# FP4 weights and rotary tables prepared beside the first scan, and a second stage whose tiles wait tile by tile

## Chip, cores and metric

The kernel runs on one core of a Trainium2 chip. A core has TensorE (PE, with its weight loads counted as PEld), VectorE (DVE), ScalarE (ACT), GpSimd (POOL) and a queue for transfers on SyncE (SP); ACT issues some transfers too. The metric is the device time of one execution in microseconds. The time before is the median of three runs; the profile is of one more execution.

## The reference, cut to what matters

The input is eight sequences of 512 tokens with 256 channels. Two layers follow each other. The first normalizes x and adds a selective state-space scan and a feed-forward net, whose inputs, weights and hidden values are quantized to FP4 in blocks of 16. The second normalizes again and adds a block-sparse attention with 16 heads and a two-layer local-attention transformer, whose queries and keys are scaled and rotated.

```python
xn = _layernorm(x)
x = x + scan(xn) + fp4_ffn(xn)                 # stage 1
xn = _layernorm(x)
x = x + sparse_attention(xn) + local_transformer(xn)   # stage 2

def step(h, inp):                              # 512 steps, state 512 x 16
    d_t, u_t, B_t, C_t = inp
    dA = jnp.exp(d_t[:, :, None] * A[None])
    h = dA * h + (d_t * u_t)[:, :, None] * B_t[:, None, :]
    return h, jnp.einsum('bdn,bn->bd', h, C_t)

def fp4_linear(x, w):                          # x @ quantized(w).T
    return jnp.einsum('bsk,nk->bsn', fp4_quant_dequant(x), fp4_quant_dequant(w))

def fp4_quant_dequant(x):                      # blocks of 16 along the last dim
    scale = jnp.maximum(jnp.max(jnp.abs(xb), -1, keepdims=True) / 6.0, 1e-12)
    return _GRID[jnp.searchsorted(_MID, jnp.abs(xb / scale))] * sign(xb) * scale

q, k = l2norm(q) * q_scale, l2norm(k) * k_scale
q = q * cos * scale + rotate_half(q) * sin * scale
k = k * cos / scale + rotate_half(k) * sin / scale
```

## The kernel before

The whole program is one launch of two stages, and each stage goes through the eight sequences (batches) one after the other. The result of stage 1 goes to a DRAM tile per batch (x1_d, stored on ACT's queue at L369), and stage 2 loads it again (load_x1, L390). All data is float32. A batch lies in tiles of 128 tokens x 256 channels, or, turned, of 128 channels x 512 tokens.

The Python program emits the instructions of all engines in one order that is written by hand; the framework then lists each engine's instructions, mostly in that order, and an engine takes its own list in order. Where two strands of work run side by side, they are generators, and `beside` (L111) takes a step of the second strand whenever its share of steps is behind that of the first. Tiles come from rotating pools. A tile that takes the bytes of an earlier one waits for the earlier one's users; the framework puts in these waits, and so a transfer's start can hang on work that has nothing else to do with it.

**Before the first scan.** The weights of stage 1 are loaded on SP's queue (`load`, L134). Then the FP4 weights are made (L177 to L213). The gate and up weights (704 x 256 each) come in four chunks each of 88 rows x 512 values, loaded on ACT's queue into q_src (two buffers). The down weight comes in two chunks of 128 x 704. `fp4` (L81) quantizes a chunk in ten instructions: on DVE the blocks' maximum (L96), the scale (L97), its reciprocal (L98, L100), on POOL the scaling (L101), on ACT the power-of-two step (L105), on DVE three more (L106 to L108), and on POOL the scaling back (L109). PE turns a chunk into a PSUM tile (ps_w at L186, ps_i at L202), and DVE or ACT, in turns, copy it out (`evac`, L46). Then head(0) runs.

**head(b)** (L218) loads x, normalizes it, turns it (xt), and computes for four channel chunks the input product (ps_in), the convolution (cv, one L235 and three L239 on DVE) and its Silu on ACT (u). Then it computes the products that give B and C (ps_xp, copied to xd at L250 and stored to a DRAM tile bc_d on SP's queue, L252), and for each chunk the step size delta and du (a softplus chain over ACT, DVE at L267 and L268, and POOL at L270 to L272).

**scan(b)** (L323) goes through two pairs of channel chunks and, in each, 16 states. For a state, one transfer spreads B and C over the partitions (bc, L330). For each chunk of the pair, ACT makes da in PSUM (L338), DVE multiplies du with B (hh, L340) and runs the recurrence over the 512 tokens in one instruction (L341), POOL multiplies with C (L342), and PE adds the states up in a PSUM bank (y, L343). After a pair, the output is gated (DVE L355, POOL L358); after both, PE projects it (ps_o, L364), DVE adds it to xs (L368) and xs is stored (L369).

**ffn(b)** (L276) quantizes xn (one chunk for two token tiles), and for each of the four token tiles computes the gate and up products, quantizes the hidden tile h (704 wide), turns it and multiplies with the down weight (L317), and adds it to x in xs (L320).

Beside each scan run ffn of the same batch and head of the next:

```python
for b in range(NB):
    rest = [ffn(b)] + ([head(b + 1)] if b + 1 < NB else [])
    beside(scan(b), chain(*rest), 34, 24)
```

So 34 steps of the scan carry 24 other steps.

**Stage 2** opens seven new pools (L380 to L386) over the space of stage 1's. SP's queue then issues, in the order of the program: wq, wk, wv, their biases, wao, bsum (to which POOL adds a bias at L403), the mask (L419; POOL fills other tiles before it, and DVE casts the mask in eight copies at L422 and L423), and for each of the two transformer layers the rotary table (512 KB, tab at L432), the two scales (qs, L435), 26 small DVE instructions that multiply them (L437 and L440 to L442), a store of the product to a DRAM tile (L444) and four small loads. `fetch` (L453) then loads the first transformer weights (wqkv, tab, wo, wf1, wf2, 5204 KB), and only then does the first proj load x1s_0.

**proj(b)** (L489) normalizes a batch (statistics at L496 and L497, the scaled values at L500), turns it to s0, and computes queries and keys of the sparse attention (ps_qk L514, copied to qt and kt by DVE at L518) and the values (ps_v L524, bias added at L529). **smax** (L535) computes the scores once (ps_s L557 and L559) to take row maxima on DVE (nm, L563 and L565). qkv, attn and ffn of the transformer and st and outer of the sparse attention follow. The order ahead of the first of them is:

```python
fetch(0, 0, "wqkv", "tab", "wo", "wf1", "wf2")
tc.keep_in_program_order(act.preload_act_table_set("natural_log_exp_and_others"))
alone(proj(0))
alone(smax(0, 0))
```

Of the kernel before, what the change touches and what calls it, by code (L numbers as in the profile page):

```python
# [38 lines left out]
def tile_kernel(ctx: ExitStack, tc: tile.TileContext, a: dict, out: bass.AP):  # L39
# [99 lines left out]
    def chunks(w):  # L139
        return w.rearrange("(k p) n -> p k n", p=P)  # L140
# [4 lines left out]
    with ExitStack() as s0:  # L145
# [28 lines left out]
        w_g = w0.tile([P, KC, FI], FP, name="w_g")  # L174
        w_u = w0.tile([P, KC, FI], FP, name="w_u")
        w_d = w0.tile([P, NI, D], FP, name="w_d")
        for name, dst in (("w_gate", w_g), ("w_up", w_u)):  # L177
            src = a[name].rearrange("(j p) d -> p j d", p=FB)
            for j in range(0, FI // FB, 2):
                raw = q.tile([P, FI], FP, tag="q_src", name="q_src")[:FB, : 2 * D]  # L180
                act.dma_start(raw.rearrange("p (j d) -> p j d", j=2), src[:, j : j + 2, :])
                fp4(raw, raw, FB, 2 * D, q, sm)
                ps = pmm.tile([P, L], FP, tag="mm", name="ps_w")
                for k in range(KC):
                    for i in range(2):
                        pe.transpose(  # L186
                            ps[:, (2 * k + i) * FB : (2 * k + i + 1) * FB],
                            raw[:, i * D + k * P : i * D + (k + 1) * P],
                            ident[:FB, :FB],
                        )  # L190
                evac(
                    dst[:, :, j * FB : (j + 2) * FB],
                    ps[:, : 4 * FB].rearrange("p (k n) -> p k n", k=KC),
                )

        def inner_to_partitions(src, dst):

            for c0, c1 in ((0, 4), (4, NI)):
                ps = pmm.tile([P, L], FP, tag="mm", name="ps_i")
                for c in range(c0, c1):  # L200
                    n = min(P, FI - c * P)
                    pe.transpose(ps[:n, (c - c0) * P : (c - c0 + 1) * P], src[:, c * P : c * P + n], ident)  # L202
                full = c1 - c0 - (c1 * P > FI)
                evac(dst[:, c0 : c0 + full, :], ps[:, : full * P].rearrange("p (c n) -> p c n", n=P))
                if c0 + full < c1:
                    n = FI - (c1 - 1) * P
                    evac(dst[:n, c1 - 1, :], ps[:n, full * P : (full + 1) * P])

        for r in range(D // P):
            raw = q.tile([P, FI], FP, tag="q_src", name="q_src")  # L210
            act.dma_start(raw, a["w_down"][r * P : (r + 1) * P, :])
            fp4(raw, raw, P, FI, q, sm)
            inner_to_partitions(raw, w_d[:, :, r * P : (r + 1) * P])  # L213


        made = {}
# [156 lines left out]
            pass  # L373
        for b in range(NB):
            rest = [ffn(b)] + ([head(b + 1)] if b + 1 < NB else [])
            beside(scan(b), chain(*rest), 34, 24)


    with ExitStack() as s1:
        w0 = s1.enter_context(tc.tile_pool(name="w1", bufs=1))  # L380
        w1 = s1.enter_context(tc.tile_pool(name="io1", bufs=2))
        sm = s1.enter_context(tc.tile_pool(name="sm1", bufs=4))
        one = s1.enter_context(tc.tile_pool(name="one1", bufs=1))
        rot = s1.enter_context(tc.tile_pool(name="rot1", bufs=2))
        pmm = s1.enter_context(tc.tile_pool(name="pmm1", bufs=6, space=PSUM))
        po = s1.enter_context(tc.tile_pool(name="po1", bufs=2, space=PSUM))  # L386

        def load_x1(b):
            t = w1.tile([P, NT, D], FP, tag="x1", name=f"x1s_{b}")
            sp.dma_start(t, x1_d[b])  # L390
            return t

        wq = load(w0, chunks(a["wq"]), [P, KC, NH * HP], "wq")
        wk = load(w0, chunks(a["wk"]), [P, KC, NH * HP], "wk")
        wv = load(w0, chunks(a["wv"]), [P, KC, D], "wv")
# [30 lines left out]
            "wqkv": [P, KC, 3 * IN], "tab": [P, 4, NT, LD], "wo": [P, IN // P, D],  # L426
            "wf1": [P, KC, 2 * HID], "wf2": [P, NHC, D],
        }
        lng, lnb, b1, b2c, tab_d = [], [], [], [], []
        for l in range(DEPTH):  # L430
            tab = one.tile(shapes["tab"], FP, tag="tab", name="tab")
            sp.dma_start(tab, a["rotary"])  # L432
            for i, name in ((0, "q_scale"), (2, "k_scale")):
                qs = sm.tile([P, LD], FP, tag="qs", bufs=2, name="qs")
                sp.dma_start(qs, a[name][l].unsqueeze(0).to_broadcast([P, LD]))  # L435
                if i == 0:
                    dve.tensor_scalar(qs, qs, 8.0, None, ALU.mult)  # L437
                hd = LD // 2
                for t in range(NT):
                    dve.tensor_tensor(tab[:, i, t, :], tab[:, i, t, :], qs, ALU.mult)  # L440
                    dve.tensor_tensor(tab[:, i + 1, t, :hd], tab[:, i + 1, t, :hd], qs[:, hd:], ALU.mult)
                    dve.tensor_tensor(tab[:, i + 1, t, hd:], tab[:, i + 1, t, hd:], qs[:, :hd], ALU.mult)  # L442
            tab_d.append(dram.tile(shapes["tab"], FP, tag=f"tab_{l}", bufs=1, name=f"tab_{l}"))
# [43 lines left out]
        x1s, ss_, bs = {}, {}, {}  # L487

        def proj(b):  # L489
            x1 = x1s[b] = load_x1(b)  # L490
            xn = one.tile([P, NT, D], FP, tag="hn", name="xn")
            st = sm.tile([P, NT, 6], FP, tag="ln_st", bufs=2, name="ln_st")
            mv = sm.tile([P, NT, 2], FP, tag="ln_mv", bufs=2, name="ln_mv")
            rs = sm.tile([P, NT], FP, tag="ln_rs", bufs=2, name="ln_rs")
            for t in range(NT):
                dve.bn_stats(st[:, t, :], x1[:, t, :])  # L496
                dve.bn_aggr(mv[:, t, :], st[:, t, :])  # L497
            inv_sqrt(rs, mv[:, :, 1], eps_t)
            for t in range(NT):
                dve.tensor_scalar(  # L500
                    xn[:, t, :], x1[:, t, :], mv[:, t, 0:1], rs[:, t : t + 1], ALU.subtract, ALU.mult
                )
            yield
            s = ss_[b] = stream("s0", "s0")
            to_channels(xn, s[:, :, S0:], pmm, "mm")
            yield
            qt = one.tile([P, 4, L], FP, tag="bqt", name="qt")
            kt = one.tile([P, 4, L], FP, tag="bkt", name="kt")
            bs[b] = qt, kt
            for dst, wt, bias, sc in ((qt, wq, bq, 0.25), (kt, wk, bk, 1.0)):  # L510
                for c in range(4):
                    ps = pmm.tile([P, L], FP, tag="mm", name="ps_qk")
                    for k in range(KC):
                        pe.matmul(  # L514
                            ps, wt[:, k, c * P : (c + 1) * P], s[:, k, S0:],
                            start=(k == 0), stop=(k == KC - 1),
                        )
                    dve.tensor_scalar(dst[:, c, :], ps, bias[:, c : c + 1], sc, ALU.add, ALU.mult)  # L518
                    yield
            for t in range(0, NT, 2):  # L520
                ps = pmm.tile([P, L], FP, tag="mm", name="ps_v")
                for i in range(2):
                    for k in range(KC):
                        pe.matmul(  # L524
                            ps[:, i * D : (i + 1) * D], s[:, k, S0 + (t + i) * P : S0 + (t + i + 1) * P], wv[:, k, :],
                            start=(k == 0), stop=(k == KC - 1),
                        )
                for i in range(2):
                    dve.tensor_tensor(  # L529
                        bv_t[:, t + i, :, :HD], ps[:, i * D : (i + 1) * D].rearrange("p (h d) -> p h d", d=HD),  # L530
                        bv.rearrange("p (h d) -> p h d", d=HD), ALU.add,
                    )
                yield
# [465 lines left out]
```

## Time and profile before

| | |
|---|---|
| median of 3 runs | 4184.37 us (4177.97 to 4188.32) |
| the profiled execution | 4182.33 us, of which the span of its instructions is 4180.5 us |
| PE / PEld busy | 3488.5 us (83%) / 1700.7 us (41%) |
| DVE busy | 2892.1 us (69%) |
| ACT busy | 1721.5 us (41%) |
| POOL busy | 1456.9 us (35%) |
| mean granted PE clock | 0.883 of full speed |
| moved by DMA | 239.27 MB, mean 57 GB/s |

The busy share is a mean over stages that differ. The page's second part cuts the span into 40 slices of 104.5 us and gives each engine's busy share in tenths: DVE's digits are 9 from the third to the seventeenth slice, where PE's are 7, and from the nineteenth slice on PE's are 9 (8 in two) while DVE's are 4 to 6. So each stage is read for itself. In a row of the groups, the line number says where the instruction is written, "out<-in" names the tiles, xN counts instructions, then come their busy time and mean duration, and last the engine's idle time just before them and what ended it. In the chain of waits, each row is what the next one waited for, with its start and duration in microseconds. In the list of issues (part 6), the last number is the median time from a transfer's issue to its landing. The first 106.2 us pass before the first scan instruction, the eight scans take until 1808, and the first matmul of stage 2 follows at about 1848.

### The profile page before, as it was taken

Reading aid. Unit: us, or ns where it says so; the run is one execution under the profiler, and the core shown is the slowest. Engines: PE = TensorE matmul, PEld = TensorE weight load, DVE = VectorE, ACT = ScalarE, POOL = GpSimd, SP = SyncE. Lnnn points to the kernel's source line nnn. Section 1 sums busy time; section 2 is a strip of 40 time slices with the busy share of each in tenths; the row PEclk is TensorE's granted clock in tenths of the full one; section 3 lists DMA queues with packets and bytes.
Section 4 is the critical chain, followed back from the end, with each engine's and each line's share of the span. In section 5 each row is a group of like instructions: output and inputs, shape, how many; then the busy total and the mean of one; then the engine's idle time right before and its main releaser. Section 6 shows DMA issues by size and latency. Waiting matters only on the chain.

```text
span 4180.5 us, 40473 instructions
## 1 busy us (share of the span) xinstructions
PE 3488.5 (83%) x13932; PEld 1700.7 (41%) x13932; DVE 2892.1 (69%) x4825; ACT 1721.5 (41%) x3411; POOL 1456.9 (35%) x1059
## 2 busy tenths in 40 slices
PE   3677777777777777759999999999989999999998
PEld 1233333333333333324454544554554544445445
DVE  6899999999999999955545545654555455456454
ACT  2454545555454545414423333343243244234333
POOL 2666665657575757521111120111021011101211
PEclk9777787787887888879999999999999999999999
DMA  2333233333332323330111010010011101110100
GB/s 63 76 81 91 77 90 80 87 81 86 78 88 80 87 76 90 80 120 26 42 37 37 31 57 26 26 52 30 27 52 42 37 26 42 36 47 26 47 27 6
DMA packets 121606, 239.27 MB, mean 57 GB/s; under 512 B 10025, under 2 KB 41769, under 8 KB 121401
## 3 DMA queue, kind: packets, MB, share of 16 engines
q1 hardware_dynamic: 118464, 230.32, 19.7%
q10 hardware_dynamic: 2936, 6.36, 0.4%
q8 instruction: 111, 1.82, 0.2%
q14 instruction: 95, 0.77, 0.1%
HBM read 226.69 MB, written 9.96 MB: 57 GB/s over the span
## 4 chain that ended last, share of the span: by engine, by line
PE 46%; DVE 10%; issue 3%; ACT 2%; POOL 2%; DMA 1%; SPq 0%; POOLq 0%; DVEq 0%; ACTq 0%
PE ps_qkv L683 8%; PE ps_g L853 5%; PE ps_a L853 4%; PE ps_qk L514 3%; PE ps_wo L815 3%; PE ps_y L888 2%; PE ps_w L871 2%; PE ps_st L609 2%; PE lo L787 2%; PE ps_ls L735 2%; PE pt_qk L674 2%; DVE pr L764 2%; DVE nm L745 1%; PE pt L773 1%; DVE hh L341 1%
## 5 line engine op out<-in xcount | busy, mean ns | idle before, releaser
L343 PE MATMUL y<-hh,ident 128*128 128x512 f32 x1024 | 692.3, 789 | 407.5 <-POOL hh L342 406.1
L342 POOL TENSOR_TENSOR hh<-hh,bc 128x512 f32<-128x512 f32 x512 | 754.0, 1482 | 553.9 <-issue 130.3
L341 DVE TENSOR_TENSOR_SCAN hh<-da,hh 128x512 f32<-128x512 f32 x512 | 609.4, 1205 | 1.9 <-ACT da L338 1.2
L340 DVE TENSOR_TENSOR hh<-du,bc 128x512 f32<-128x512 f32 x512 | 575.6, 1145 | 32.8 <-PE y L343 23.8
L338 ACT ACTIVATE da<-delta,a_neg 128x512 f32<-128x512 f32 x512 | 349.3, 689 | 488.4 <-DVE hh L341 486.6
L343 PEld LDWEIGHTS y<-hh,ident 128*128 128x128 f32 x1024 | 204.1, 231 | 813.1 <-POOL hh L342 739.9
L702 POOL TENSOR_TENSOR r<-r,r 128x512 f32<-128x512 f32 x128 | 162.8, 1272 | 385.4 <-DVE r L700 385.4
L751 ACT ACTIVATE pr<-ps_ls,nm 128x256 f32<-128x256 f32 (+1 forms) x512 | 221.7, 446 | 176.7 <-DVE nm L745 176.6
L860 DVE SCALAR_TENSOR_TENSOR ht<-ps_a,b,gl 128x512 f32<-128x512 f32 x96 | 72.0, 750 | 264.1 <-PE ps_a L853 261.2
L463 POOL MEMSET sa<- 128x1 f32 x16 | 1.6, 98 | 725.4 <-DVE sa L819 386.2
L698 DVE TENSOR_TENSOR r<-ps_qkv,tab 128x512 f32<-128x512 f32 x128 | 87.9, 686 | 220.6 <-ACT sq L697 220.6
L853 PE MATMUL ps_g<-hn,wf 128*128 128x512 f32 (+1 forms) x384 | 212.1, 671 | 24.9 <-issue 24.3
L859 ACT ACTIVATE gl<-ps_g,b 128x512 f32<-128x512 f32 x96 | 65.9, 686 | 392.3 <-PE ps_g L853 392.3
L697 ACT ACTIVATE sq<-ps_qkv 128x512 f32<-128x512 f32 x128 | 76.6, 598 | 293.2 <-PE ps_qkv L683 293.2
L853 PE MATMUL ps_a<-hn,wf 128*128 128x512 f32 (+1 forms) x384 | 197.1, 634 | 0.0
L613 ACT ACTIVATE pt_e<-ps_st 128x512 f32<-128x512 f32 (+1 forms) x384 | 172.8, 536 | 15.2 <-PE ps_st L607 14.6
L745 DVE TENSOR_REDUCE nm<-ps_ls 128x2 f32<-128x512 f32 (+1 forms) x256 | 147.5, 618 | 44.7 <-PE ps_ls L735 43.8
L683 PE MATMUL ps_qkv<-wqkv,s 128*128 128x512 f32 x384 | 174.7, 604 | 0.0
L683 PE MATMUL ps_qkv<-wqkv,sf 128*128 128x512 f32 x384 | 173.4, 601 | 0.0
L764 DVE TENSOR_SCALAR pr<-pr,lrs 128x256 f32<-128x256 f32 (+1 forms) x512 | 148.7, 332 | 4.8
L338 ACT ACT_TABLE_LOAD x115 | 147.5, 1283 | 5.8 <-DVE hh L341 3.8
L735 PE MATMUL ps_ls<-lkt,lqt 64*128 64x256 f32 (+1 forms) x1024 | 140.0, 396 | 0.0
(212 smaller groups left out, 6450.8 us busy)
## 6 DMA issues: line engine op xcount, KB each, us to landing
bc<-bc_d SPq DMA_DIRECT2D x256, 512.0 KB, 4.9
wqkv<-in_wqkv SPq DMA_DIRECT2D x16, 1536.0 KB, 6.4
wf<-in_wf SPq DMA_DIRECT2D x16, 1364.0 KB, 5.9
wf<-in_wf SPq DMA_DIRECT2D x16, 768.0 KB, 4.8
tab<-tab SPq DMA_DIRECT2D x18, 512.0 KB, 4.3
wo<-in_wo SPq DMA_DIRECT2D x16, 512.0 KB, 3.9
x<-in_x SPq DMA_DIRECT2D x8, 512.0 KB, 5.4
x<-xs ACTq DMA_DIRECT2D x8, 512.0 KB, 5.8
```

Source lines behind the costliest of these rows:

```text
L338: act.activation(da, delta[:, c, :], AF.Exp, scale=a_neg[:, c, n : n + 1])
L340: dve.tensor_tensor(hh, du[:, c, :], bc[:, 0, :], ALU.mult)
L341: dve.tensor_tensor_scan(hh, da, hh, 0.0, ALU.mult, ALU.add)
L342: pool.tensor_tensor(hh, hh, bc[:, 1, :], ALU.mult)
L343: pe.matmul(ys[i], ident, hh, start=(n == 0), stop=(n == NS - 1))
L613: act.activation(pt[:, :n], banks[g][:, :n], AF.Exp)
L683: pe.matmul(ps, shifted(s, k, t * P, P), wqkv[:, k, i * IN : (i + 1) * IN], start=(k == 0), stop=(k == KC - 1),)
L735: pe.matmul(banks[r][:, i * nk : (i + 1) * nk], qt[LD * r : LD * (r + 1), 2 * p + i, w * P : (w + 1) * P], kt[LD * r : LD * (r + 1), 2 * p ...
L745: dve.tensor_reduce(nm, banks[r][:, : 2 * nk].rearrange("p (g n) -> p g n", g=2), AX.X, ALU.max, negate=True)
L751: act.activation(pr[:, at], banks[r][:, at], AF.Exp, bias=nm[:, i : i + 1], accum_out=rs[:, i : i + 1],)
L764: dve.tensor_scalar(pr[:, at], pr[:, at], rs[:, i : i + 1], None, ALU.mult)
L853: pe.matmul(dst[:m], wf1[:, k, off + c * P : off + c * P + m], hn[:, k, :], start=(k == 0), stop=(k == KC - 1),)
```

## The change

**FP4 weights.** The loops that make the FP4 weights become a generator, `fp4_weights`, with ten steps. They no longer stand ahead of head(0) but run beside the first scan, ahead of ffn(0), which needs them.

**Rotary tables.** The tables of the two transformer layers are made in another generator, `rotary_tables`, with two steps, in stage 1's pools. Each table takes 2 x 4 products over all token tiles at once and one scaling of the q scales; in the kernel before it took 2 x 12 products and the scaling. The generator runs after head(1) beside the first scan. With the two generators, the first scan's 34 steps carry 36 other steps instead of 24.

**Second stage.** Its seven pools get `reuse_waits="tile"`: a new tile waits for the users of the tiles whose bytes it takes, and for no others. The first x1s load is emitted ahead of the loads of stage 2's weights, and the first fetch of transformer weights after proj(0).

```diff
-        for name, dst in (("w_gate", w_g), ("w_up", w_u)):
...
-        for r in range(D // P):
...
+        def fp4_weights():
+            for name, dst in (("w_gate", w_g), ("w_up", w_u)):
+                src = a[name].rearrange("(j p) d -> p j d", p=FB)
+                for j in range(0, FI // FB, 2):
+                    raw = q.tile([P, FI], FP, tag="q_src", name="q_src")[:FB, : 2 * D]
+                    act.dma_start(raw.rearrange("p (j d) -> p j d", j=2), src[:, j : j + 2, :])
+                    fp4(raw, raw, FB, 2 * D, q, sm)
+                    ps = pmm.tile([P, L], FP, tag="mm", name="ps_w")
...
+                    yield
+            for r in range(D // P):
+                raw = q.tile([P, FI], FP, tag="q_src", name="q_src")
+                act.dma_start(raw, a["w_down"][r * P : (r + 1) * P, :])
+                fp4(raw, raw, P, FI, q, sm)
+                inner_to_partitions(raw, w_d[:, :, r * P : (r + 1) * P])
+                yield
+
+        tab_d = [dram.tile([P, 4, NT, LD], FP, tag=f"tab_{l}", bufs=1, name=f"tab_{l}") for l in range(DEPTH)]
+
+        def rotary_tables():
+
+            for l in range(DEPTH):
+                tab = one.tile([P, 4, NT, LD], FP, tag="tab", name="tab")
+                sp.dma_start(tab, a["rotary"])
+                for i, name in ((0, "q_scale"), (2, "k_scale")):
+                    qs = sm.tile([P, LD], FP, tag="qs", bufs=2, name="qs")
+                    sp.dma_start(qs, a[name][l].unsqueeze(0).to_broadcast([P, LD]))
+                    if i == 0:
+                        dve.tensor_scalar(qs, qs, 8.0, None, ALU.mult)
+                    hd = LD // 2
...
+                    lo, hi = slice(0, hd), slice(hd, LD)
+                    for at, cols, sc in ((i, lo, lo), (i, hi, hi), (i + 1, lo, hi), (i + 1, hi, lo)):
+                        dve.tensor_tensor(tab[:, at, :, cols], tab[:, at, :, cols], by(sc), ALU.mult)
+                sp.dma_start(tab_d[l], tab)
+                yield
...
             rest = [ffn(b)] + ([head(b + 1)] if b + 1 < NB else [])
-            beside(scan(b), chain(*rest), 34, 24)
+            if b == 0:
+                rest = [fp4_weights(), *rest, rotary_tables()]
+            beside(scan(b), chain(*rest), 34, 24 if b else 36)
...
-        w0 = s1.enter_context(tc.tile_pool(name="w1", bufs=1))
...
+        w0 = s1.enter_context(tc.tile_pool(name="w1", bufs=1, reuse_waits="tile"))
...
+        x1_first = load_x1(0)
         wq = load(w0, chunks(a["wq"]), [P, KC, NH * HP], "wq")
...
-        lng, lnb, b1, b2c, tab_d = [], [], [], [], []
+        lng, lnb, b1, b2c = [], [], [], []
         for l in range(DEPTH):
-            tab = one.tile(shapes["tab"], FP, tag="tab", name="tab")
...
-            sp.dma_start(tab_d[l], tab)
...
-            x1 = x1s[b] = load_x1(b)
+            x1 = x1s[b] = load_x1(b) if b else x1_first
...
-        fetch(0, 0, "wqkv", "tab", "wo", "wf1", "wf2")
         tc.keep_in_program_order(act.preload_act_table_set("natural_log_exp_and_others"))
         alone(proj(0))
+        fetch(0, 0, "wqkv", "tab", "wo", "wf1", "wf2")
         alone(smax(0, 0))
```

In the program as built, the framework moves some of this: two FP4 chunks and the rotary tables come ahead of head(0)'s work on DVE, and the other eight chunks stand between the first scan's instructions. On SP's queue the tables' transfers stand behind x_1's load and ahead of bc_d's store.

More of the change, by code (lines that the diff above doesn't have):

```diff
@@ L176, in tile_kernel @@
         w_d = w0.tile([P, NI, D], FP, name="w_d")
-        for name, dst in (("w_gate", w_g), ("w_up", w_u)):
[L178 to L194, printed above, removed]
         def inner_to_partitions(src, dst):
@@ L207, in inner_to_partitions @@
                     evac(dst[:n, c1 - 1, :], ps[:n, full * P : (full + 1) * P])
-        for r in range(D // P):
[L210 to L213, printed above, removed]
+        def fp4_weights():
[6 more added lines that the diff above has]
+                    ps = pmm.tile([P, L], FP, tag="mm", name="ps_w")
+                    for k in range(KC):
+                        for i in range(2):
+                            pe.transpose(
+                                ps[:, (2 * k + i) * FB : (2 * k + i + 1) * FB],
+                                raw[:, i * D + k * P : i * D + (k + 1) * P],
+                                ident[:FB, :FB],
+                            )
+                    evac(
+                        dst[:, :, j * FB : (j + 2) * FB],
+                        ps[:, : 4 * FB].rearrange("p (k n) -> p k n", k=KC),
+                    )
+                    yield
[5 more added lines that the diff above has]
+                yield
@@ new lines, in tile_kernel, with by @@
+        tab_d = [dram.tile([P, 4, NT, LD], FP, tag=f"tab_{l}", bufs=1, name=f"tab_{l}") for l in range(DEPTH)]
[9 more added lines that the diff above has]
+                    hd = LD // 2
+                    def by(cols):
+                        return qs[:, cols].unsqueeze(1).to_broadcast([P, NT, hd])
+                    lo, hi = slice(0, hd), slice(hd, LD)
[3 more added lines that the diff above has]
+                yield
@@ L375, in tile_kernel @@
             rest = [ffn(b)] + ([head(b + 1)] if b + 1 < NB else [])
-            beside(scan(b), chain(*rest), 34, 24)
+            if b == 0:
+                rest = [fp4_weights(), *rest, rotary_tables()]
+            beside(scan(b), chain(*rest), 34, 24 if b else 36)
     with ExitStack() as s1:
-        w0 = s1.enter_context(tc.tile_pool(name="w1", bufs=1))
[L381 to L386, printed above, removed]
+        w0 = s1.enter_context(tc.tile_pool(name="w1", bufs=1, reuse_waits="tile"))
+        w1 = s1.enter_context(tc.tile_pool(name="io1", bufs=2, reuse_waits="tile"))
+        sm = s1.enter_context(tc.tile_pool(name="sm1", bufs=4, reuse_waits="tile"))
+        one = s1.enter_context(tc.tile_pool(name="one1", bufs=1, reuse_waits="tile"))
+        rot = s1.enter_context(tc.tile_pool(name="rot1", bufs=2, reuse_waits="tile"))
+        pmm = s1.enter_context(tc.tile_pool(name="pmm1", bufs=6, space=PSUM, reuse_waits="tile"))
+        po = s1.enter_context(tc.tile_pool(name="po1", bufs=2, space=PSUM, reuse_waits="tile"))
         def load_x1(b):
@@ L428, in tile_kernel @@
         }
-        lng, lnb, b1, b2c, tab_d = [], [], [], [], []
+        lng, lnb, b1, b2c = [], [], [], []
         for l in range(DEPTH):
-            tab = one.tile(shapes["tab"], FP, tag="tab", name="tab")
[L432 to L443, printed above, removed]
-            sp.dma_start(tab_d[l], tab)
             lng.append(load(w0, a["lng"][l], [P, KC], f"lng{l}"))
```

## Prediction

> **What bounds the kernel now.** First the busy times cut into four stretches, one row each: length, then busy time and instruction count of PE, PEld, DVE, ACT and POOL, then granted PE clock, DMA share, GB/s.
>
> ```profile
> 0.00:106.00 106.00, 37.81 (x96) 17.73 (x96) 66.73 (x140) 30.09 (x47) 32.31 (x34) 0.91 0.23 63
> 106.00:1808.00 1702.00, 1256.84 (x2828) 553.36 (x2828) 1569.16 (x1817) 870.62 (x1132) 1070.26 (x730) 0.80 0.33 83
> 1808.00:1848.00 40.00, 0.00 (x0) 0.00 (x0) 10.63 (x72) 1.79 (x3) 4.16 (x12) 0.56 0.80 265
> 1848.00:4180.00 2332.00, 2193.88 (x11008) 1129.63 (x11008) 1245.59 (x2798) 819.00 (x2230) 350.20 (x284) 0.95 0.10 35
> ```
>
> Four regimes: a start with no engine full, the scans with DVE at 92%, a gap of 40 us without one matmul, and the second stage with PE at 94%. The change touches the start, the first scan and the gap. In the built program the other seven scans and everything from the second stage's first smax on keep their order on every engine; I carry their times over.
>
> Second, where the start ends: the timeline at the scan's first instruction, and the groups before it (instruction, shapes, count | busy us, mean ns | idle before it).
>
> ```profile
> L107 DVE TENSOR_TENSOR q_v<-q_v,q_m 88x512 f32<-88x512 f32 x8 | 7.1, 890 | 0.4
> L108 DVE TENSOR_TENSOR q_v<-q_v,q_m 88x512 f32<-88x512 f32 x8 | 5.8, 722 | 0.1
> L96 DVE TENSOR_REDUCE q_amax<-q_src 88x32 f32<-88x512 f32 x8 | 5.5, 682 | 9.6 <-DMA q_src<-in_w_gate 7.7 <-DMA q_src<-in_w_up 1.9
> ...
> 106.20 1.74 DVE L340 TENSOR_TENSOR hh<-du,bc 128x512 f32<-128x512 f32 x1 [3.84 <-POOL du L272]
> ```
>
> DVE works 66.7 of 106.2 us: 39.5 idle, mostly hops of an FP4 chunk from DVE to POOL, ACT, DVE, POOL, PE and back. Third, the chain of waits through the gap (start, us, what).
>
> ```profile
> 1808.04 4.83 DMA wq<-in_wq
> 1812.89 4.94 DMA bsum<-in_bao
> ...
> 1824.78 8.58 DMA tab<-tab
> 1833.38 3.52 DMA tab<-in_rotary
> ...
> 1840.24 4.85 DMA x1s<-x
> ...
> 1850.49 2.08 PE ps_qk L514 x2
> ```
>
> No arithmetic holds the gap but SP's queue: the x1s load that the first layernorm needs stands behind two round trips of the rotary table. Fourth, how much room the scan leaves.
>
> ```profile
> L341 DVE TENSOR_TENSOR_SCAN hh<-da,hh 128x512 f32<-128x512 f32 x448 | 533.9, 1205 | 1.6 <-ACT da L338 1.2
> L340 DVE TENSOR_TENSOR hh<-du,bc 128x512 f32<-128x512 f32 x449 | 503.4, 1142 | 19.7 <-PE y L343 17.4 <-DMA bc<-bc_d 2.0
> ```
>
> **The Trainium skill.** "SBUF — State Buffer", Who interferes with whom: a DVE instruction with two SBUF inputs contends with a GpSimd instruction that reads SBUF, one with at most one SBUF input (outside two-port modes) does not. The trace agrees: L341, with da in PSUM, stays at 1.21 us; L340, two SBUF inputs, takes 0.68 us undisturbed and 1.14 on average. So moved POOL work is not free. "Perfetto Trace Analysis", Optimization Strategy: regimes with different busiest engines may gain by interleaving. Here both are DVE's, so only idle time can be gained. "DMA: Bandwidth & Descriptors", Issuing engines are not separate DMA queues: all transfers share the same 16 engines. The gap's ten two-microsecond rows from 1826 to 1846 together moved 7.0 MB in 20 us, 351 GB/s; I price transfers with that.
>
> **Part 1: FP4 weights leave the start.** In the built program two chunks are still quantized at once (q_src has two buffers), then DVE goes on with both layernorms, the table products and head(0). x lands for DVE at 13.9 us as before. From there: four bn_stats, four bn_aggr and the pending L108, 2.8 us; x_1's statistics 2.0; two table products and four L69, 2.4; transposes and the xt copy, so xt at about 22.5 instead of 73. Before, the xt copy at 72.64 led to the first L340 at 106.20: 33.6 us of convolution, softplus chain and POOL. The chain is kept, plus 1 us for table products in it: first scan instruction at **57 us, 49 us earlier**.
>
> What comes back, into scan 0, is DVE work. Undisturbed means: an 88-row chunk is L96 0.68, L97 0.17, L98 0.34, L100 0.17, L106 0.29, L107 0.69, L108 0.69 = 3.03 us; a 704-wide one 3.8; evacuations 3.3 in all. Moved: 6x3.03 + 2x3.8 + 2.8 = 28.6; the quantization of xn and a copy, which go with it, 6.7. Sum 35.3 us. With them go 20 POOL instructions (12 of 88 rows, 4 of 704, 4 for xn). A POOL instruction costs DVE 0.41 us in the scan: L340's excess 0.46x64 plus 8 us for L267, L268 and the small ones is 38 us per batch, over some 92. So 8.2 more: 43.5.
>
> How true such a sum is, the last batch shows, which has no next head: its second L355 comes 191.0 us after the previous batch's, where the others stand 215.1 apart. A head is 21 us of DVE undisturbed and 12 POOL instructions: 25.9 by this rule, 24.1 measured, 0.93. So 40.5, and 2.5 for in-order stalls: 43. **Net 6 us gained.** Bounds: 13 gained (the scan's idle absorbs more), 8 lost (stalls of 14 us more). ACT at 51% and PE at 74% of that stretch take their shares (0.6 and 0.9 us per chunk) beside it; were they full, the chunks' hops would cost what rival 3 says. The q_src loads (176 KB each) hide under bc traffic at 83 GB/s.
>
> **Part 2: rotary tables.** 52 DVE instructions become 20. They leave the gap, where they cost little themselves (0.10 to 0.14 us each in a row) but two loads, two stores and four small loads on SP. Though traced after head(1), they are built at the front: on SP right behind x_1's load, ahead of bc_d. Twenty times about 0.2 us is 4 us, 3 beside waits for PE, 1 on the chain (counted). SP is held there for the products, then for tab_0's store (3.9 us by the gap's second store) before it reloads the buffer, and tab_1's store must wait for the last products at about 40 us. bc_d's store needs xd at 41, so nothing is late; margin of the second reload before its product: 3 us. Bound: 0 to 5 us lost.
>
> **Part 3: the gap.** T is the end of the last ps_o (1808.0). SP now issues b2l when a late hh is done, wq after the last ps_z, then wk, wv and x1s_0, all some 14 us before T; x1s_0 needs about 8. So the layernorm starts behind identb at T+0.75, not 1845.11. From statistics to ps_qk took 5.4 us: T+6.1. Now other things are late.
>
> First, eight mask casts stand on DVE ahead of qt's evacuation. Their load waits for POOL's bsum, whose load waits for the last xs store: 0.5+5.8, bsum 2.3, POOL 0.75, raw_mask 0.4+2.1, casts 1.2: T+13. PE has six PSUM banks and is six tiles in (12 us) only at T+18, so nothing stops. ps_v's additions end 20.0 us after ps_qk's start: T+26.1.
>
> Second, six statistics instructions on x1s_1 now stand on DVE ahead of the first nm reduction, for which ps_s's banks and PE wait. x1s_1 is issued behind wqkv, tab, wo, wf1 and wf2: 5204 KB, 5.33 MB. wqkv leaves at T+11.7, bytes flow 2 us later (as after 1824.25), 15.2 us at 351 GB/s: landing T+28.8. Between 290 and 430 GB/s: T+32 to T+26. With 1.6 us of statistics, nm starts at T+30.4; before:
>
> ```profile
> 1870.82 4.88 DVE L565 TENSOR_REDUCE nm<-ps_s 128x2 f32<-128x512 f32 x8 [0.30 <-PE ps_s L559]
> ```
>
> That is T+62.8. **Gain 32.4 us**, bounds 25 (store or loads late) and 37 (no stall). wqkv has landed well before ps_qkv needs it. With 40 us of idle gone PE also loses less to the clock, 0.50 from 1816 to 1850: two microseconds, hidden by x1s_1 and not counted.
>
> **Sum.** 6 + 32.4 = 38.4. The profiled execution took 4182.33 us (span 4180.5 and 1.8 around it): 4143.9. The median of the runs is 2.0 higher: **4146 us**, 0.9% less. What a measurement of this kernel can tell from no change is about 0.3%, 12.6 us.
>
> **Rivals.** 1: the start only moves. Scan 0 grows by what it saves or 8 more, the gap is gained: 4152 to 4160. For it: DVE is at 92% and both regimes are DVE's. Against: 39.5 idle us at the start. 2: the gap moves to x1s_1 and the masks. The xs store, bsum and raw_mask are three waits in a row, each before the second stage's 5.33 MB; if each lands 3 us later and bytes flow at 290 GB/s, nm starts at T+42, gain 20: 4158. For it: bsum took 4.94 us in the old gap; against: that was under 1.9 MB of loads now done. The same time results if x1s_0 was not freed early. 3, **slower**: DVE runs in order, so each late chunk stops it at its hops. Alone, ten chunks took 66 us, 6.6 each against 3.5 of DVE, 3.1 exposed; if POOL is also behind an hh of 1.48 at both its turns, 6 us per chunk. Eight chunks: 49 us above 43, the start loses 43, 4195. It decides from 4.8 us per chunk, where scan 0 has grown by 82. Against: between a chunk's hops the built order has two or three scan instructions of 0.7 to 1.2 us, as for ffn's own quantization, which waited 6.8 us in all. 4: the tables' SP waits hold bc_d and the first scan by 10 us: 4156.
>
> **Numbers.** My forecast 0.66, rival 1 0.15, rival 2 0.09, rival 3 0.04, rival 4 0.06. All bounds at their good end gain 13+37 = 50: 4134, and 4129 with the runs' own spread of 5 us. All at their bad end gain 25-8-5 = 12: 4172; as three independent bounds are hardly all at their worst, I take 4168, which holds rivals 1, 2 and 4; rival 3 is left out. Faster by over 0.3% (below 4171.8) 0.91, within 0.05, slower 0.04.
>
> **What would show it.** First scan product at 57 us (beyond 65: rival 4). First pair of y additions of scan 0 at about 200 us, was 206.6 and 210.0; at 250, rival 3; at 210, rival 1. Later pairs 215.1 apart. PE idle between ps_o and the first transpose about 5 us, was 40.2. DVE idle before the second x1s statistics of 0 to 6 us, ended by its load, and nm at T+30; at T+40 rival 2. A shift in the later second stage, whose order is unchanged, would prove my carrying over wrong.

## The result and the profile after

The changed kernel takes 4163.7 us (median of 13 runs, 4150.95 to 4170.22); the kernel before took 4177.63 us in the runs beside them. The ratio is 0.9966, with an interval of 0.995 to 0.9982: about 14 us faster, where 38 were forecast. The profiled execution has a span of 4164.2 us against 4180.5.

The stretches of the changed kernel, cut at the first scan product and at the second gating instruction (u, DVE) of each pair of channel chunks, so that a row is half a scan. The columns are those of the prediction's first view.

```profile
0.00:51.35 51.35, 23.24 (x48) 8.68 (x48) 30.22 (x82) 20.52 (x30) 9.29 (x15) 0.85 0.44 137
51.35:182.63 131.28, 72.47 (x124) 25.42 (x124) 124.88 (x155) 47.02 (x67) 88.28 (x63) 0.58 0.28 75
182.63:288.89 106.26, 80.70 (x175) 36.26 (x176) 91.97 (x102) 43.25 (x57) 61.54 (x41) 0.74 0.24 68
288.89:438.54 149.65, 105.87 (x254) 48.84 (x254) 120.39 (x156) 73.14 (x97) 78.25 (x55) 0.82 0.27 72
438.54:549.87 111.33, 83.31 (x177) 34.03 (x178) 105.90 (x119) 68.09 (x87) 73.05 (x50) 0.82 0.30 79
549.87:656.55 106.68, 76.48 (x184) 36.45 (x182) 94.99 (x117) 44.80 (x60) 62.71 (x43) 0.79 0.34 85
```

The same for the kernel before:

```profile
0.00:106.20 106.20, 37.81 (x96) 17.73 (x96) 66.73 (x140) 30.29 (x48) 32.51 (x35) 0.90 0.23 62
106.20:209.98 103.78, 69.23 (x144) 29.61 (x144) 91.96 (x100) 48.63 (x64) 67.44 (x46) 0.76 0.33 78
209.98:321.73 111.75, 85.15 (x177) 34.37 (x178) 105.08 (x119) 68.36 (x88) 73.44 (x51) 0.79 0.31 79
321.73:425.07 103.34, 75.29 (x184) 36.22 (x183) 94.55 (x117) 44.25 (x59) 61.65 (x42) 0.78 0.33 88
425.07:536.83 111.76, 85.34 (x177) 34.33 (x178) 105.11 (x120) 68.34 (x88) 73.91 (x51) 0.79 0.30 79
536.83:639.93 103.10, 74.41 (x184) 35.68 (x183) 94.39 (x116) 44.34 (x59) 61.66 (x42) 0.80 0.34 88
```

The start is 54.9 us shorter. Scan 0's first half is 27.5 us longer, its second half 5.5 shorter, and the first half of scan 1 is 46.3 us longer. From the end of the last row on, the scans take the same time but for 1.1 us: the last pair of scan 7 is gated at 1820.66 instead of 1802.90. So the first stage, which holds the FP4 weights and the tables, lost **17.8 us**.

What stands in the long row is seen in the timeline of DVE (start, duration, instruction, idle before it and what ended it):

```profile
288.89 0.75 DVE L380 SCALAR_TENSOR_TENSOR u<-u,d_par,y 128x512 f32<-128x512 f32 x1 [1.39 <-PE y L368]
...
294.26 0.41 DVE L345 TENSOR_TENSOR xs<-x,ps_d 128x256 f32<-128x256 f32 x1
294.74 0.69 DVE L50 COPY xt<-ps_tr 128x512 f32<-128x512 f32 x1
...
297.51 0.81 DVE L260 TENSOR_SCALAR cv<-ps_in,conv_w,conv_b 128x512 f32<-128x512 f32 x1
...
317.01 0.43 DVE L292 TENSOR_SCALAR w<-e 128x512 f32<-128x512 f32 x1 [3.82 <-ACT e L291]
...
324.67 1.74 DVE L365 TENSOR_TENSOR hh<-du,bc 128x512 f32<-128x512 f32 x1 [4.83 <-POOL du L297]
```

Scan 0 ends at 288.89. ffn(0) adds its last token tile (L345) only then, and right behind it comes all of head(1): transposed x, convolution, softplus chain. The first scan product of batch 1 is at 324.67, 35.8 us after scan 0's last gating. In the kernel before, ffn(0) was done at 252, head(1) followed it there too but lay between the instructions of scan 0, which ran until 321.73, and the next scan product came 1.8 us after that:

```profile
252.02 0.39 DVE L320 TENSOR_TENSOR xs<-x,ps_d 128x256 f32<-128x256 f32 x1
252.33 0.68 DVE L50 COPY xt<-ps_tr 128x512 f32<-128x512 f32 x1
...
256.04 0.79 DVE L235 TENSOR_SCALAR cv<-ps_in,conv_w,conv_b 128x512 f32<-128x512 f32 x1
...
257.76 1.09 DVE L340 TENSOR_TENSOR hh<-du,bc 128x512 f32<-128x512 f32 x1
```

The gap gained. The chain of waits of the changed kernel (start, us, what):

```profile
1825.77 0.42 DVE xs L393
1826.22 3.84 DMA x<-xs
...
1838.72 13.61 DMA x1s<-x
...
1853.89 0.60 DVE nm L579
```

And DVE's timeline at the three places the prediction names:

```profile
1826.24 0.75 DVE L510 BATCH_NORM_STATS2 ln_st<-x1s 128x6 f32<-128x256 f32 x2
...
1836.17 0.23 DVE L450 CAST mask<-raw_mask 128x128 bf16<-128x128 f32 x1 [5.07 <-DMA raw_mask<-in_mask]
...
1852.36 0.76 DVE L510 BATCH_NORM_STATS2 ln_st<-x1s 128x6 f32<-128x256 f32 x2 [1.37 <-DMA x1s<-x]
...
1853.81 2.47 DVE L579 TENSOR_REDUCE nm<-ps_s 128x2 f32<-128x512 f32 x4
```

With T the end of the last ps_o, where the last addition to xs starts (1825.77; 1808.0 before), the layernorm starts at T+0.5, and the first nm reduction is at T+28.0, where it was at T+62.8: **34.8 us gained**. From nm to the end of the span both kernels take the same, 2309.7 and 2310.4 us. So 17.8 lost, 34.8 gained and 0.7 lost make the 16.3 us between the spans.

### The profile page after: what moved, and what is told of

The parts are those of the page before. It is cut to its first block, busy times and chain, and to the rows that moved or that the text cites. A ratio compares the mean times of both kernels' runs of the same rounds, so it can differ in the third digit from the quotient of the medians.

```text
span 4164.2 us, 40399 instructions
## 1 busy us (share of the span) xinstructions
PE 3502.5 (84%) x13916; PEld 1700.5 (41%) x13932; DVE 2896.4 (70%) x4793; ACT 1715.0 (41%) x3404; POOL 1460.2 (35%) x1059
## 4 chain that ended last, share of the span: by engine, by line
PE 45%; DVE 10%; issue 3%; ACT 2%; POOL 2%; DMA 1%; SPq 0%; POOLq 0%; DVEq 0%; ACTq 0%
PE ps_qkv L697 8%; PE ps_g L867 5%; PE ps_a L867 4%; PE ps_wo L829 3%; PE ps_qk L528 3%; PE ps_y L902 2%; PE ps_w L885 2%; PE ps_st L623 2%; PE lo L801 2%; PE ps_ls L749 2%; PE pt_qk L688 2%; DVE pr L778 2%; DVE nm L759 1%; PE pt L787 1%; DVE hh L366 1%
## 5 line engine op out<-in xcount | busy, mean ns | idle before, releaser
L368 PE MATMUL y<-hh,ident 128*128 128x512 f32 x1024 | 708.1, 804 | 434.7 <-POOL hh L367 432.9
L759 DVE TENSOR_REDUCE nm<-ps_ls 128x2 f32<-128x512 f32 (+1 forms) x256 | 147.4, 618 | 45.3 <-PE ps_ls L749 44.4
```

Of the source, the lines that this page charges most:

```text
L368: pe.matmul(ys[i], ident, hh, start=(n == 0), stop=(n == NS - 1))
L759: dve.tensor_reduce(nm, banks[r][:, : 2 * nk].rearrange("p (g n) -> p g n", g=2), AX.X, ALU.max, negate=True)
```

## The experiments

Two theories on the loss. **S**: the work beside scan 0 is a serial chain (FP4 chunks, ffn(0), head(1)), now longer than scan 0, so that a head comes late and the scan waits. **W**: the moved work fills DVE and POOL and costs its time wherever it stands. The table has the moments of each profiled execution: the first scan product, the second pair of scan 0, the second pair of scan 7, and the first nm counted from the last xs addition. Each ratio is to runs of the kernel before that were taken beside it. e8 and e9 leave work out and are told below.

| kernel | first product | scan 0 | scan 7 | nm | median us | ratio to before (interval) |
|---|---|---|---|---|---|---|
| before | 106.2 | 321.7 | 1802.9 | 62.8 | 4177.6 | |
| changed | 51.4 | 288.9 | 1820.7 | 28.0 | 4163.7 | 0.9966 (0.995 to 0.9982) |
| e1 FP4 alone | 52.9 | 286.8 | 1829.5 | 63.2 | 4200.8 | 1.0057 (1.0036 to 1.0079) |
| e2 gap and tables | 106.3 | 336.2 | 1813.7 | 28.2 | 4154.1 | 0.9941 (0.9919 to 0.9963) |
| e3 gap alone | 104.8 | 322.7 | 1807.6 | 33.4 | 4148.7 | 0.993 (0.9909 to 0.9951) |
| e4 head(1) first | 54.2 | 289.2 | 1822.8 | 28.1 | 4158.8 | 0.9965 (0.9948 to 0.9981) |
| e5 ffn late | 51.1 | 273.4 | 1824.1 | 28.2 | 4200.9 | 1.0074 (1.0046 to 1.0101) |
| e6 tables last | 106.0 | 326.4 | 1809.2 | 28.1 | 4150.3 | 0.9928 (0.9907 to 0.995) |
| e7 early loads | 106.4 | 322.0 | 1803.2 | 29.4 | 4143.5 | 0.9925 (0.9898 to 0.9952) |
| e10 FP4 with head(0) | 73.1 | 312.0 | 1811.0 | 29.3 | 4137.6 | 0.991 (0.9879 to 0.9942) |
| e11 pace 80 | 51.5 | 284.0 | 1827.5 | 28.5 | 4172.0 | 0.999 (0.9974 to 1.0006) |
| e12 e7, FP4 moved | 53.3 | 287.1 | 1832.2 | 29.3 | 4161.5 | 0.9959 (0.9944 to 0.9974) |

**e1, the FP4 weights alone.**

```diff
 # kernel before, with fp4_weights() of the change
-    beside(scan(b), chain(*rest), 34, 24)
+    if b == 0:
+        rest = [fp4_weights(), *rest]
+    beside(scan(b), chain(*rest), 34, 24 if b else 34)
```

> Only the FP4 weights move beside the first scan; tables and second stage stay as before. Theory S (the strand beside scan 0 is a serial chain, FP4 chunks, then ffn(0), then head(1), and it is longer than the scan, so head(1)'s convolution and softplus run in the open after scan 0's last pair): the first scan product at about 50 us, head(1)'s first convolution on DVE after scan 0's second pair of y additions, the last pair of the last scan 15 to 20 us later than before's 1802.9, time about 18 us over before, ratio 1.003 to 1.005. Rival W (the moved work simply fills DVE and POOL): the same total, but the added time lies evenly over scans 0 and 1 with DVE above 93% busy there. The forecast on record (net gain of 6 us): ratio 0.9985.

The last pair came 26.6 us later than before's, more than the 15 to 20 expected, and the ratio says slower. The move on its own costs time; the forecast of 0.9985 is excluded. The added time isn't spread evenly, as W had it: after scan 0's last gating 44.4 us pass without a scan product.

**e2, the gap and the tables alone.**

```diff
 # changed kernel
+for _ in fp4_weights():
+    pass
 made = {}
...
-        rest = [fp4_weights(), *rest, rotary_tables()]
-    beside(scan(b), chain(*rest), 34, 24 if b else 36)
+        rest = [*rest, rotary_tables()]
+    beside(scan(b), chain(*rest), 34, 24 if b else 26)
```

> The changed kernel with the FP4 weights made at the start again; tables beside the first scan and the second stage as in the changed kernel. Both theories: scans end within 5 us of before's 1808, the first nm reduction follows the last ps_o by 28 us as in the changed kernel (62.8 before), so about 35 us less than before, less 0 to 4 for the tables in stage 1: ratio 0.992. If part of the gap's gain came from the first scan's new timing, the ratio is above 0.995.

The gap's gain came as expected (nm at 28.2), but the scans ended 10.8 us later than before's, not within 5, and the ratio lay above the 0.992 expected.

**e3, the second stage's waits alone.** The table loop stays in stage 2 and the FP4 weights at the start.

```diff
 # kernel before; likewise for the other six pools of stage 2
-        w0 = s1.enter_context(tc.tile_pool(name="w1", bufs=1))
+        w0 = s1.enter_context(tc.tile_pool(name="w1", bufs=1, reuse_waits="tile"))
...
+        x1_first = load_x1(0)
         wq = load(w0, chunks(a["wq"]), [P, KC, NH * HP], "wq")
...
-        fetch(0, 0, "wqkv", "tab", "wo", "wf1", "wf2")
...
         alone(proj(0))
+        fetch(0, 0, "wqkv", "tab", "wo", "wf1", "wf2")
```

> Only the second stage's pools wait tile by tile, with the x1s_0 load first and the fetch after proj(0); the tables stay in the gap and the FP4 weights at the start. If the two round trips of the table on SP's queue still count, they now hold back the fetch and x1s_1 behind it: the first nm 40 to 50 us after the last ps_o, gain 13 to 22 us, ratio 0.995 to 0.997. If moving the tables bought nothing (they are hidden behind proj(0)), nm at 28 us and ratio 0.992.

nm came at 33.4, between the two expectations. The larger part, 29 us of 34.8, comes from the pools, the early x1s_0 load and the later fetch; which of these three gives how much was not separated. The other 5.4 us are not all the tables' own. In e3 the layernorm starts only at T+4.4 instead of T+0.5, as x1s_0 lands later: it is issued behind b2l, which waited on SP's queue until the last y addition of scan 7 was done. The rest, 1.5 us, fits the tables: DVE waits 4.0 us for the load of the second table, whose products stand in its list ahead of the last additions to ps_v and of nm.

**e4, head(1) ahead of the FP4 weights.**

```diff
-        rest = [fp4_weights(), *rest, rotary_tables()]
+        rest = [rest[1], fp4_weights(), rest[0], rotary_tables()]
```

> The changed kernel with one edit: beside scan 0 run head(1), then the FP4 weights, then ffn(0). Theory S: the stretch without scan instructions after scan 0 (38 us in the changed kernel) goes, some of it comes back as ffn(0) trailing into scan 1; the last pair of the last scan 20 to 45 us earlier than the changed kernel's 1820.7, time 25 to 40 us under the changed kernel: ratio to before 0.987 to 0.991. Rival W (work fills DVE and POOL wherever it stands): no change against the changed kernel, ratio 0.996 to 0.998.

S's number was missed, and W's was met: the last pair came 2.2 us later than the changed kernel's, and the ratio is 0.9965 against 0.9966. Still, the time went as S says. The stretch after scan 0 went, but ffn(0) ran on into scan 1, and after scan 1's second pair, which this view of DVE begins with, the scan waited for head(2):

```profile
529.67 0.75 DVE L380 SCALAR_TENSOR_TENSOR u<-u,d_par,y 128x512 f32<-128x512 f32 x1 [1.67 <-PE y L368]
534.92 1.74 DVE L365 TENSOR_TENSOR hh<-du,bc 128x512 f32<-128x512 f32 x1 [2.50 <-POOL du L297]
...
553.71 1.41 DVE L365 TENSOR_TENSOR hh<-du,bc 128x512 f32<-128x512 f32 x1 [6.88 <-POOL du L297]
```

So the late work is handed to the next batch, and this order within scan 0 doesn't remove it.

**e5, ffn one batch late.**

```diff
-    rest = [ffn(b)] + ([head(b + 1)] if b + 1 < NB else [])
...
+    if b == 0:
+        rest, n = [fp4_weights(), head(1), rotary_tables()], 22
+    elif b + 1 < NB:
+        rest, n = [ffn(b - 1), head(b + 1)], 24
+    else:
+        rest, n = [ffn(b - 1), ffn(b)], 28
+    beside(scan(b), chain(*rest), 34, n)
```

> The changed kernel with ffn one batch later: beside scan 0 run the FP4 weights and head(1); beside scans 1 to 6 ffn of the batch before and head of the next; beside scan 7 ffn(6) and ffn(7). All arithmetic is the same. Theory S (the 24.5 us of idle DVE time that the changed kernel has more in the first scans come from a side strand that is longer than scan 0, so head(1) and head(2) come late): the idle goes, the second pair of scan 6 ends at 1600 to 1614 (before 1611.9, changed 1629.9), and scan 7, which has two ffn beside it, gives 20 to 40 us back, so the time is 4160 to 4180. Rival W (the moved work costs that much wherever it stands): the second pair of scan 6 at 1625 to 1632.

The second pair of scan 6 came at 1600.5, inside S's range, but that doesn't decide: an ffn is still owed there, and each later batch took 222 us in this order where it took 215; why isn't shown. The stretch after scan 0 was gone (102.1 us for the first half of scan 1, 149.7 in the changed kernel). The time, 4200.9, missed its range of 4160 to 4180, and the kernel is slower than before.

**e6, e7.** e6 is e2 with the tables' generator chained beside scan 7 and scan 0's pace back at 24 in 34. e7 adds earlier loads.

```diff
 # e6, from e2
-    rest = [ffn(b)] + ([head(b + 1)] if b + 1 < NB else [])
-    if b == 0:
-        rest = [*rest, rotary_tables()]
-    beside(scan(b), chain(*rest), 34, 24 if b else 26)
+    rest = [ffn(b)] + ([head(b + 1)] if b + 1 < NB else [rotary_tables()])
+    beside(scan(b), chain(*rest), 34, 24)
```

```diff
 # e7, from e6
+x1_second = load_x1(1)
+raw = rot.tile([P, L], FP, tag="gl", bufs=3, name="raw_mask")[:, : 2 * P]
...
+sp.dma_start(raw, a["mask"].rearrange("m p n -> p m n"))
 wao = load(w0, chunks(a["wao"]), [P, KC, D], "wao")
```

> FP4 weights at the start and the second stage as in e2, but the tables' generator is chained beside scan 7, so that scan 0 keeps its pace of 24 other steps in 34. In the built order the tables' products still stand at the front of DVE's list, so only the pace differs from e2. If the 10.8 us that e2 lost in scans 0 to 2 come from the pace (26 in 34 gives the planner another order): the last pair of scan 7 at 1803 to 1807, nm 28 us after the last ps_o, ratio 0.991 to 0.993. If they come from the tables' own instructions and transfers: 1811 to 1815, ratio 0.994.

> e6 with the loads of x1s_1 and of the mask issued right after x1s_0 and the value bias, the mask into another buffer. If the waits on the mask (5 us) and on x1s_1 (1.4 us, and 1.6 us of statistics) are what is left of the gap: the first nm 19 to 23 us after the last ps_o instead of 28, 6 to 8 us less than e6, ratio 0.989 to 0.991. If the banks and the clock of TensorE hold it: 26 to 28 us and no difference to e6.

e6 ended its scans 6.3 us after before's, between its two expectations, and e7 0.3, with the same order of stage 1 on DVE. So a single profile's scans are known to some 6 us, and of e2's 10.8 us the part that its pace costs stays open; the tables themselves cost nothing that e7 shows. In e7 masks and x1s_1 no longer wait, yet nm came at 29.4, later than both expectations. Its chain of waits:

```profile
1805.10 7.89 DMA x1s<-x
...
1818.17 15.03 PE ps_qk L529 x32
1833.21 3.45 PE ps_v L539 x16
...
1837.77 2.48 DVE nm L580 x4
```

TensorE works through from 1818.17 to nm, and x1s_0 landed 4.7 us after the start of the last xs addition, where e6's had landed before it. SP's queue waited longer ahead of x1s_0, for b2l, in e7 (first line) than in e6 (waited for, us in total, times, longest):

```profile
SPq L434 <- PE y L370: 9.8, 1, 9.8
```

```profile
SPq L430 <- POOL hh L369: 2.5, 1, 2.5
```

So two things cancel. From the first statistics to nm e7 took 24.7 us and e6 27.6: the early loads did gain 2.9 us, and the later x1s_0 took 4.2. What is left of e7's gap is the first load, 5 us of layernorm and 20 us in which TensorE has no pause. With x1s_0 as early as in e6, nm would come at about T+25.2, an estimate from these two runs. Why b2l's place comes free later in e7 and in e3 wasn't followed up.

**e8, e9, a shorter chain beside scan 0.** Both leave out ffn(0), and batch 0's scan then adds to x itself (this edit isn't shown); e9 makes the FP4 weights at the start, e8 beside scan 0.

```diff
-        rest = [fp4_weights(), *rest, rotary_tables()]
-    beside(scan(b), chain(*rest), 34, 24 if b else 36)
+        rest = [fp4_weights(), rest[1], rotary_tables()]    # e9: without fp4_weights()
+    beside(scan(b), chain(*rest), 34, 24 if b else 22)      # e9: 12
```

> The changed kernel with ffn(0) left out (batch 0 gets no feed-forward part; all else is computed), FP4 weights beside scan 0, so that the strand there is ten FP4 chunks and head(1). To be read against e9, which differs from it only in where the FP4 weights are made. Theory S (strand too long for scan 0): without ffn(0) the strand fits, no stretch without scan instructions follows scan 0, and moving the weights gains: 55 us at the start less some 47 us of DVE work, so the last pair of scan 7 ends 3 to 13 us earlier than in e9. Rival W (the moved work costs more than the start saves wherever it stands): 5 to 20 us later than in e9.

> e8 with the FP4 weights at the start (ffn(0) left out here too). Beside scan 0 runs head(1) alone. Expected: first scan product at 106 us, scan 0 shorter than before's 215.5 by the DVE work of ffn(0), 45 to 60 us. The comparison with e8 is stated there.

The last pair of scan 7 was at 1765.86 in e8 and at 1763.95 in e9. Without ffn(0), moving the weights costs 1.9 us, less than single profiles can tell, and the medians of four runs each, 4103.5 and 4102.3, can't tell the two apart either; with ffn(0), the changed kernel ends 17.5 us after e7 and e12 29.0 after e7. That is neither expectation: S named a gain, W at least 5 us of loss. e9's own was missed too: scan 0 took 180.7 us, 35 less than before's, where 45 to 60 were expected. The sums of the stretches to the end of scan 2's first pair, e8 first:

```profile
sum 599.46, PE 395.96 PEld 160.56 DVE 539.98 ACT 280.73 POOL 359.16; mean PE 65.99 PEld 26.76 DVE 90.00 ACT 46.79 POOL 59.86
```

```profile
sum 601.09, PE 383.51 PEld 159.62 DVE 532.18 ACT 281.40 POOL 350.51; mean PE 63.92 PEld 26.60 DVE 88.70 ACT 46.90 POOL 58.42
```

DVE is idle for 59.5 us in e8 and for 68.9 in e9, so some of the start's idle time is won; but DVE is busy for 7.8 us more, and as both do the same work, its instructions take longer when they run side by side. Two things follow. With ffn(0) out of the way no stretch without scan products follows scan 0 (1.8 us in e8), and most of the loss is gone, as S says; but leaving out ffn(0) also takes work off DVE and POOL, and the two were not separated. And even then nothing is won, as W says.

**e10, the FP4 weights beside head(0).**

```diff
 # e7
-for _ in fp4_weights():
-    pass
...
-for _ in head(0):
-    pass
+beside(head(0), fp4_weights(), 10, 10)
```

> e7 with one edit: the FP4 weights run beside head(0), ahead of the scan, a chunk for each of its ten steps, so that two chains of hops share the start and nothing is added to scan 0's strand. If the start's 39.5 us of idle DVE time are hops that the other chain can fill: first scan product at 75 to 90 us instead of 106, some FP4 work still inside scan 0, last pair of scan 7 10 to 25 us before e7's 1803.2, ratio 0.986 to 0.990. If work in the start can't overlap, or comes back in scan 0 as in the changed kernel: within 5 us of e7, ratio 0.992.

The first product came at 73.1, so two chains of hops do share the start: it shrank by 33.3 us. But scan 0's second pair was only 10.0 us ahead of e7's, and the last pair of scan 7 was 7.8 behind, outside both expectations. Part of the FP4 work still lay in scan 0. The intervals of e10 and e7 overlap. This result S doesn't explain. ffn(0) was done at 249.2 and head(1) followed it well inside scan 0, as in e7; the next scan product came 0.7 us after scan 0's last gating. Yet up to the end of scan 2's first pair, at 640.2 in both kernels, DVE's busy time in the scans is 10.8 us longer than in e7 and its idle time 22.5. So all of the start's gain can be lost again without a late head. Why isn't settled: the waits of its first scans are many, of 1 to 3 us, on PE and ACT.

**e11, the pace.**

```diff
-    beside(scan(b), chain(*rest), 34, 24 if b else 36)
+    beside(scan(b), chain(*rest), 34, 24 if b else 80)
```

> The changed kernel with the pace of the side strand beside scan 0 at 80 steps in 34 instead of 36, so that all of it is emitted within the first 16 of scan 0's 34 steps. If the stretch without scan instructions after scan 0 comes from the pace (head(1) emitted too late): it goes, the last pair of scan 7 is 15 to 30 us earlier than 1820.7, ratio 0.990 to 0.993. Theory S (each link of the strand waits for the one before, so an earlier place in the program changes nothing): head(1) still follows scan 0's last pair, last pair of scan 7 within 6 us of 1820.7, ratio 0.995 to 0.998.

The pace isn't it: head(1) stayed behind scan 0's last pair, with the next scan product at 320.27 (324.67 in the changed kernel). The last pair of scan 7 was 6.8 us later than the changed kernel's, just outside S's range, and so was the ratio. What holds head(1) there isn't shown. It uses no result of ffn(0); it is written behind it, both take their PSUM tiles in turn from the same four (mm), and the framework sets the lists of the engines. e4 shows that the order of writing counts.

**e12, the move repeated on e7.**

```diff
-for _ in fp4_weights():
-    pass
...
-    beside(scan(b), chain(*rest), 34, 24)
+    if b == 0:
+        rest = [fp4_weights(), *rest]
+    beside(scan(b), chain(*rest), 34, 24 if b else 34)
```

> e7 with one edit: the FP4 weights beside scan 0, 34 steps in 34. It repeats the moving of the weights alone, now beside the shortened gap. If the move costs what the changed kernel showed against e7 (17.5 us at the end of the scans): last pair of scan 7 at 1817 to 1830, ratio to before 0.995 to 0.999. If the loss in e1 and in the changed kernel hung on the old gap or the tables: within 5 us of e7, ratio 0.992.

The last pair came at 1832.16, 29.0 us after e7's, 2 us beyond the range. The loss doesn't hang on the old gap. e1 with 26.6 and e12 agree; the changed kernel, with 36 steps in 34, lost some 10 less. Most of that is the stretch after scan 0, of 35.8 us instead of 44.4 and 44.5; why isn't shown.

**The lowest medians** are those of e7 and e10. Both are faster than before, and their medians are 20 and 26 us below the changed kernel's; e10's interval lies below the changed kernel's, e7's just touches it. They keep the second stage's part and leave the FP4 weights ahead of the scan. The intervals of e3 and e6 overlap with theirs: the second stage's waits alone, with no work moved (e3), gain all that these measurements can tell.

## Why the prediction was wrong

The direction and the second stage were right. The measured 4163.7 lies between the stated 4129 and 4168, but that is partly luck: the first stage lost 17.8 us, more than the 13 that parts 1 and 2 allowed at their worst, and the runs of before, too, had moved down. The gain is a third of the forecast, by one term of part 1.

**The start.** Forecast 57 us, measured 51.35. x's transposed copy came at 19.9 instead of 22.5, and the chain behind it took 31.5 us. Rival 4 (bc_d held by the tables) did not happen.

**What comes back: the step that failed.** It was put at 43 us: 43.5 of DVE work, times 0.93, and 2.5 for in-order stalls. From first product to last pair the scans grew by 72.6. In the rows above, up to the end of scan 2's first pair, DVE's busy time in the scans rises from 491.1 to 538.1 us, 47.0, close to the 43.5 that the instructions and the POOL contention gave. Its idle time there rises from 42.6 to 67.1: 24.4 us, where the sum had 2.5 and its bound 14. The factor of 0.93 took 3 us off and was wrong in sign. The stalls are not at the FP4 chunks' hops: between 51.35 and 182.63 DVE is idle for only 6.4 of 131 us. Of the 24.4, 20.5 lie in the first half of scan 1, where head(1) runs after scan 0's end; another 7.6 lie in the second half of scan 0, which were not followed up, and the first half has 5.4 less. The sign that was to show this, scan 0's first pair at about 200 us, came early, at 179.0 and 182.6: it watched a stretch in which nothing went wrong. The sum added up work and never asked how long the chain beside scan 0 is: FP4 chunks to about 156 us, ffn(0) from there at some 30 us a token tile to 294, and then head(1). The built order showed head(1)'s convolution behind scan 0's last u on DVE; the prediction read only the chunks' places in it.

The experiments bound this account: in e4, where head(1) comes first, and in e10, where no head is late, the start's gain was lost again all the same. That the stalls were left out is shown; that a shorter chain alone would have kept the 6 us is not.

**The rivals.** Rival 1 (the start only moves; scan 0 grows by what it saves or 8 more) was nearest: the scans grew by 18 more. Its time, 4152 to 4160, was still too low. Rival 3 named the growth but not the mechanism: it put the stall on the chunks' hops. Rival 2 (gap to T+42) did not happen.

**Part 2.** The tables cost nothing in stage 1 within what e7 shows (last pair 0.3 us later). In the gap, nm came 5.4 us earlier with them moved (e3 against the changed kernel), most of it by an earlier x1s_0; in the total times of e3 and e6, which differ in the tables alone, no gain is seen. The counts were off: 50 DVE instructions (25 for each layer, not 26) became 18, not 52 and 20.

**Part 3.** Forecast nm at T+30.4 and 32.4 us gained; measured T+28.0 and 34.8. The masks were cast by T+11.5 (forecast T+13), x1s_1 landed at T+26.6 (T+28.8), and TensorE did not stop for the late masks. The term for PE's clock, two microseconds that were not counted, hardly showed: the clock was 0.83 in the first 12 us of matmuls before (1850 to 1862) and 0.84 in the changed kernel's from 1829 to 1840. The second stage behind nm took 0.7 us more; that two executions agree so well is partly chance, as the last section shows.

**The sum.** 6 forecast and -17.8 measured for part 1 (with the tables), 32.4 and 34.8 for part 3. The runs of before beside the changed kernel's had a median 6.7 us below that of the three runs that the forecast started from, which brought the measured time that much nearer to 4146.

## What to carry to other kernels

Work moved beside a loop has a length as well as a sum: follow the chain of the work beside the loop to its end, and ask whether what the next iteration needs still comes before the loop's last instruction; where it doesn't, reordering within the iteration may only pass the delay on (e4). The length isn't the whole price: in e10 no head came late, and the start's gain was still lost again. If the loop's engine is already busy for over nine tenths, moving that engine's work into it can win no more than the idle time that goes from where the work stood (39.5 us of DVE in the start became 21.1), and the same work may take longer beside the loop (7.8 us in e8 against e9). Waits on whole pools at a border between stages can cost more than they seem to, since they hold the first loads of the next stage behind the last work of the one before; with the first load issued early and a later fetch, waiting tile by tile gained 29 us in e3.

## What was not expected of the hardware

The second stage has the same matmuls in every kernel here, and from the first nm to the end of the span it took 2288 us in e9 and 2314 in e6. Those 26 us are more than this whole change moved, and they come between executions: the 16 runs of e6 alone lie 39 us apart. PE's busy time in the stage was 2147.94 and 2175.02 us for as many matmuls, its mean granted clock 0.96 and 0.95 of full speed, while DVE's busy time was 1232.88 and 1235.42. So a part of the change is read better from a stage's own moments in the profile than from the total time.
